# Gated delta rule block: projecting the four batches as two pairs, and storing each batch's decays with one transfer

## The chip, the cores and the metric

The kernel runs on one core of a Trainium2 chip, as one launch. The metric is the device time of that launch in microseconds (us). A core has five engines that each take their instructions in a fixed order: TensorE (PE, matmuls and transposes), VectorE (DVE), ScalarE (ACT), GpSimd (POOL) and SyncE (SP, which here only issues transfers). ACT and POOL issue transfers too; in the profile, the queue side of an engine carries a q (SPq, ACTq, POOLq). PE accumulates into PSUM, of which this kernel makes banks of 128 × 512 floats; everything else lives in SBUF, or is passed through tensors in device memory.

## The reference, cut to what matters

One transformer block over 4 batches of 512 tokens, 512 channels wide, all in float32: attention by a gated delta rule, then a gated feed-forward layer. Both are wrapped in a normalisation that is scaled and shifted by a modulation computed from a conditioning vector c.

```python
mod = (silu(c) @ wmod).reshape(4, 6, 1, 512)
sa, ca, ga, sb, cb, gb = (mod[:, i] for i in range(6))   # |ga|, |gb| at least 0.25
h = layernorm(x) * (1 + ca) + sa
x = x + ga * attention(h)
h = layernorm(x) * (1 + cb) + sb
x = x + gb * feed_forward(h)          # (silu(h Wg^T) * (h Wu^T)) Wd^T, 2048 hidden

def attention(h):
    q = short_conv(h @ Wq)            # causal, 4 taps, then silu: 6 heads x 64
    k = short_conv(h @ Wk)            # 6 heads x 64
    v = short_conv(h @ Wv)            # 6 heads x 128
    beta = sigmoid(h @ Wb)
    g = -exp(A_log) * softplus(h @ Wa + dt_bias)        # the decays
    q, k = l2norm(q) / 8, l2norm(k)
    # per head, token by token:
    #   S = S * exp(g);  S = S + k (beta * (v - k S));  o = q S
    o = rmsnorm(o) * norm_weight * silu(h @ Wg)
    return o @ Wo
```

## The kernel before, in words

The program is one function, `adaln_block`. It writes its work down stage by stage; a scheduler then fixes one order of instructions for each engine, and the engines keep to it, so a wait in front of one instruction holds up all that stand behind it on that engine. The order of the stages in the source is the main input to that order. The lists `steps` and `tails` hold small pieces of work that are put among larger ones: `between(h)` (called in the loops of `values` and `gates`) takes the next piece of the modulation, and `lagging` puts a block's last part one block later.

Four batches pass through these stages; the letters are the functions' own.

- `load_x` (L210–222) loads the four chunks of a batch's x, 128 tokens each. Batch 0 is loaded by SP, the others by ACT's queue. One of them has a tile of its own (`room`, a slot of the tag `hf`); the others take turns in four slots `xt`.
- `normed_t` (L275–296) normalises a batch on DVE (statistics at L272 and L273, scaling at L285), transposes it on PE (16 transposes `pxt`, L291), and applies the modulation on ACT (L292). The result is `ht`; three such tiles exist.
- `decays(bs, hts)` (L313–403) computes beta and g for several batches at once: a projection `pab` (L322 for one batch, L330 for several), transposes `pat` (L338), a chain of small ACT and DVE operations, a running sum `pd` (L383) by matmul, transposes `pgt` (L396) and a copy `gyt` (L398). ACT then stores g to `gd` and y to `yd`, in four transfers for each batch (L401 and L402).
- `keys` (L447–470), `queries` and `values` (L480–485) project by blocks of 128 output channels for each batch in the list they are given: four matmuls `pp_k`, `pp_q`, `pp_v` (L417), a scaled copy on ACT (L425), three convolution taps on DVE (L427), silu on ACT (L431). `squares` adds the norms: a square on ACT (L437) and small matmuls `pn` (L443). `values` also transposes v (`pvt`, L490) and scales it on DVE (L492). `gates` (L498–510) has matmuls `pp_g` and one activation on ACT (L504), no DVE. Every block's weights, 256 KB, are loaded once per call and block.
- The modulation (L163–203) is a matmul `pm` (L185), a copy `part` on DVE (L187), a fold `pmt` (L191) and rows `pmg` (L195).
- `triangles(b)` (L515–596) prepares the delta rule of a batch: it loads the decays back, spread over the partitions (`ec`, L521; `ex`, L545 and L549), multiplies keys with keys (L563), and inverts the triangular matrices by a chain of small DVE operations (`ti`, `tip`, L580–592), whose results are stored in `td` and `ttd` and loaded as `t` and `lm`.
- `delta_rule(b)` (L758 on) goes over the 4 chunks: `operands` (L600–670, matmuls L620, L648, L656, L663, products on DVE such as `yk` at L631), `scan` (L671–701: `pf`, `pm`, and `r` and `o` back and forth between PE, ACT and DVE), `finish` (squares and products on POOL at L715 and L721, sum on DVE at L717), `project` (`pwo` at L734, `xr` on POOL at L737).
- `weight_sums` (L785–798) loads feed-forward weights, adds them on POOL and stores the sums; `feed_forward` (L800–890) uses them.

PSUM is split into three banks `fill` for the projections, three banks `seq` for the steps of the delta rule, and a scratch of two halves.

The stages stand in the source in this order (`rest` is 1, 2, 3): batch 0 is normalised; keys and queries of 0; the loads of x1 and x2; values and triangles of 0; normalise 1 and 2; gates of 0; load and normalise 3; then

```python
    rest_betas = decays(rest, hts)
    delta_rule(0)
    weight_sums()
    keys(rest, hts)
    queries(rest, hts)
    complete()
    values([1], hts)
    gates([1], hts)
    triangles(1)
    values(rest[1:], hts)
    delta_rule(1)
    gates([2], hts)
```

and the gates of 3, followed by the feed-forward layers, with the triangles and delta rules of 2 and 3 among them. So batch 0 goes alone as far as its delta rule, and the keys and queries of the three others come together.

Of the kernel before, what the change touches and what calls it, by code (L numbers as in the profile page):

```python
# [19 lines left out]
NT = T // P  # L20
# [17 lines left out]
def adaln_block(  # L38
# [52 lines left out]
        return bank("seq", 3, name)  # L91


    kd, qd, vd, sd, gd, yd, xmid = ([] for _ in range(7))
    for b in range(B):
        kd.append(dr.tile([P, NP, T], F32, name=f"kd{b}"))
        qd.append(dr.tile([P, NP, T], F32, name=f"qd{b}"))
        vd.append(dr.tile([NT, P, H, DV], F32, name=f"vd{b}"))
        sd.append(dr.tile([NT, DV, H, P], F32, name=f"sd{b}"))
        gd.append(dr.tile([2, H, NT, C + 1], F32, name=f"gd{b}"))  # L100
        yd.append(dr.tile([2, H, NT, C], F32, name=f"yd{b}"))
        xmid.append(dr.tile([T, D], F32, name=f"xmid{b}"))
    wsum = [dr.tile([NF // 2, P, 7, 2, P], F32, name=f"wsum{i}") for i in range(2)]
    gate_d = dr.tile([2, B, D], F32, name="gate_d")
# [24 lines left out]
        out=upto, in_=upto, pattern=[[1, P]], compare_op=ALU.is_ge, fill=0.0, base=0,  # L129
        channel_multiplier=-1,  # L130
    )
    far = const.tile([2 * H, NT, 1], F32, name="far")
    pool.memset(far, FAR)

    start = const.tile([P, 2, NT, C + 1], F32, name="start")
# [73 lines left out]

    def load_x(b):  # L210
        ts = []
        if b == 2:

            room = w1.tile([P, NT, D], F32, tag="hf", bufs=2, name=f"xt{b}")
        for c in range(NT):
            if b == 2:
                t = room[:, c, :]
            else:
                t = pa_.tile([P, D], F32, tag="xt", bufs=4, name=f"xt{b}_{c}")
            (act if b else sp).dma_start(t, x[b, c * P : (c + 1) * P, :])  # L220
            ts.append(t)
        return ts
# [18 lines left out]
    nw = const.tile([P, 1], F32, name="nw")  # L241
    sp.dma_start(nw, norm_weight.rearrange("(p o) -> p o", o=1))
    for t in gd:
        sp.dma_start(t.rearrange("a h c i -> (a h) c i")[:, :, 0:1], far)


    kc, qc, lm1, t11, t22, xs = ([] for _ in range(6))
# [65 lines left out]
    def decays(bs, hts):  # L313

        m = len(bs)
        n = f"{bs[0]}"
        pab = (seq if bs == [0] else fill)(f"pab{n}")
        if m == 1:

            rows = P  # L320
            for k in range(KD):
                pe.matmul(  # L322
                    pab[k * S : (k + 1) * S, :], wab[:, k, :], hts[bs[0]][:, k, :],
                    start=True, stop=True,
                )
        else:
            rows = m * S
            for k in range(KD):
                for i, b in enumerate(bs):
                    pe.matmul(  # L330
                        pab[i * S : (i + 1) * S, :], wab[:, k, :], hts[b][:, k, :],
                        start=(k == 0), stop=(k == KD - 1),
                    )
        ab = pa_.tile([P, T], F32, tag="acc", bufs=4, name=f"ab{n}")[:rows]
        act.copy(ab, pab[:rows])
        pat = (seq if bs == [0] else fill)(f"pat{n}")
        for c in range(NT):
            pe.matmul(  # L338
                pat[:, c * P : c * P + m * S], ab[:, c * P : (c + 1) * P],
                fold if m == 1 else ident[:rows, :rows], start=True, stop=True,  # L340
            )
        pv = pat.rearrange("p (c b h) -> p b c h", b=P // S, h=S)[:, :m]

        def small(nm):
            return pa_.tile([P, 3, H, NT], F32, tag=nm, bufs=1, name=f"{nm}{n}")[:, :m]

        z, e, t, t2, beta = (small(i) for i in ("z", "e", "t", "t2", "beta"))
        s = e
        gy = pa_.tile([P, 3, 2, H, NT], F32, tag="gy", bufs=1, name=f"gy{n}")[:, :m]
        for i in range(m):  # L350
            vec.tensor_tensor(
                z[:, i], pv[:, i, :, 0:H].rearrange("p c h -> p h c"),
                dtb[:, :, None].broadcast_to([P, H, NT]), ALU.add,
            )
        act.activation(beta, pv[:, :, :, H : 2 * H].rearrange("p b c h -> p b h c"), AF.Exp, scale=-1.0)
        flat = [v.rearrange("p b h c -> p (b h c)") for v in (z, e, t, t2, s, beta)]
        fz, fe, ft, ft2, fs, fb = flat
        vec.tensor_scalar_add(fb, fb, 1.0)
        vec.reciprocal(fb, fb)


        vec.scalar_tensor_tensor(fe, fz, -1.0, fz, ALU.mult, ALU.max)
        act.activation(fe, fe, AF.Exp, scale=-1.0)
        vec.tensor_scalar_add(ft, fe, 2.0)
        vec.reciprocal(ft, ft)
        vec.tensor_mul(ft, ft, fe)
        vec.tensor_mul(ft2, ft, ft)
        vec.tensor_scalar_mul(fs, ft2, 1.0 / 17.0)
        for q in (15.0, 13.0, 11.0, 9.0, 7.0, 5.0, 3.0):
            vec.scalar_tensor_tensor(fs, fs, 1.0 / q, ft2, ALU.add, ALU.mult)  # L370
        vec.scalar_tensor_tensor(fs, fs, 1.0, ft, ALU.add, ALU.mult)
        vec.tensor_scalar_max(fz, fz, 0.0)
        vec.scalar_tensor_tensor(fs, fs, 2.0, fz, ALU.mult, ALU.add)
        g, y = gy[:, :, 0], gy[:, :, 1]
        for i in range(m):
            vec.tensor_tensor(
                g[:, i], s[:, i], neg_a[:, :, None].broadcast_to([P, H, NT]), ALU.mult
            )
            vec.tensor_scalar_max(g[:, i], g[:, i], G_FLOOR)
        pd = (seq if bs == [0] else fill)(f"pd{n}")  # L380
        hc = H * NT
        for i in range(m):
            pe.matmul(  # L383
                pd[:, i * hc : (i + 1) * hc], upto, g[:, i].rearrange("p h c -> p (h c)"),
                start=True, stop=True,
            )
        act.activation(
            y.rearrange("p b h c -> p b (h c)"), pd[:, : m * hc].rearrange("p (b c) -> p b c", b=m),
            AF.Exp,
        )  # L390
        for i, b in enumerate(bs):
            for par in range(2):
                r = slice(par * C, (par + 1) * C)
                pool.tensor_copy(y8[b][r, :, par::2], y[r, i])
            pgt = (seq if bs == [0] else fill)(f"pgt{b}")
            pe.transpose(pgt[: 2 * hc, :P], gy[:, i].rearrange("p a h c -> p (a h c)"), ident)  # L396
            gyt = pa_.tile([P, T], F32, tag="acc", bufs=4, name=f"gyt{b}")[: 2 * hc, :P]
            act.copy(gyt, pgt[: 2 * hc, :P])  # L398
            for a in range(2):
                own = slice(a * C, (a + 1) * C)  # L400
                act.dma_start(gd[b][a].rearrange("h c i -> (h c) i")[:, 1:], gyt[:hc, own])  # L401
                act.dma_start(yd[b][a].rearrange("h c i -> (h c) i"), gyt[hc:, own])  # L402
        return beta

    tails, pending = [], []
# [42 lines left out]
    def keys(bs, hts):  # L448
# [1 line left out]
        for i, b in enumerate(bs):  # L450
            sk[b] = pa_.tile([P, H, NT], F32, tag=f"sk{i}", bufs=1, name=f"sk{b}")
        for p in range(NP):
            w = first_w if bs == [0] and p == 0 else weight(w_k, p, f"k{bs[0]}_{p}")
            for b in bs:
                n = f"k{b}_{p}"
                kt = conv_silu(w, cw["k"], p, hts[b], n)
                act.dma_start(kd[b][:, p, :], kt)
                lagging(lambda a=(kt, sk[b], p, 1.0, n): squares(*a))
        betas = decays(bs, hts) if bs == [0] else rest_betas

        def scalars():
            for i, b in enumerate(bs):
# [16 lines left out]
    def values(bs, hts):  # L479
        for h in range(H):  # L480
            w = weight(w_v, h, f"v{bs[0]}_{h}")
            for b in bs:
                vt = conv_silu(w, cw["v"], h, hts[b], f"v{b}_{h}")
                lagging(lambda a=(b, h, vt): by_token(*a))
                between(h)

    def by_token(b, h, vt):
        pvt = fill(f"pvt{b}_{h}")
# [9 lines left out]
    def gates(bs, hts):  # L498
        for h in range(H):
            w = weight(w_g, h, f"g{bs[0]}_{h}")  # L500
            for b in bs:
# [5 lines left out]
                )  # L507
                if tails:
                    tails.pop(0)()
                between(h)  # L510


    ex, at, td, ttd, hf = {}, {}, {}, {}, {}
# [1 line left out]
    def triangles(b):  # L515
# [4 lines left out]
        for par in range(2):  # L520
            sp.dma_start(  # L521
                ec[par * C : (par + 1) * C].rearrange("p h c i -> p (h c i)"),
                gd[b][par].rearrange("h c i -> (h c i)").partition_broadcast(C),
            )
        kp = w1.tile([P, NP, T], F32, tag="kp", bufs=1, name=f"kp{b}")
        sp.dma_start(kp, kd[b])
# [16 lines left out]
        for par in range(2):  # L543
            tok = slice(par * C, (par + 1) * C)
            sp.dma_start(  # L545
                e[(1 - par) * C : (2 - par) * C, par].rearrange("p h c i -> p (h c i)"),
                yd[b][par].rearrange("h c i -> (h c i)").partition_broadcast(C),
            )
            sp.dma_start(  # L549
                e[tok, par].rearrange("p h c i -> p (h c) i"),  # L550
# [339 lines left out]
        down(NF // NQ - 1)  # L890


    hts = {0: normed_t(0, xts)}
    keys([0], hts)
    queries([0], hts)
    rest = list(range(1, B))
    xts = {b: load_x(b) for b in rest[:2]}
    loaded = []

    def step(j):  # L900
# [3 lines left out]
            loaded.append(modulation_load(j))  # L904

    steps.extend(lambda j=j: step(j) for j in range(2, 7))
    values([0], hts)
    triangles(0)
    for b in rest[:2]:
        hts[b] = normed_t(b, xts[b])  # L910
    gates([0], hts)
    for b in rest[2:]:
        hts[b] = normed_t(b, load_x(b))
    wo = const.tile([P, H, D], F32, name="wo")
    after(wo[:1, 0, :1])
    sp.dma_start(wo, w_o.rearrange("(h p) f -> p h f", p=P))
    rest_betas = decays(rest, hts)
    delta_rule(0)
    weight_sums()
    keys(rest, hts)  # L920
    queries(rest, hts)
    complete()
    values([1], hts)
    gates([1], hts)
    triangles(1)
    values(rest[1:], hts)
    delta_rule(1)
    gates([2], hts)
    complete()
    gates([3], hts)  # L930
# [60 lines left out]
```

## Time and profile before

| what | value |
|---|---|
| median of 3 runs | 1337.42 us (1333.15 to 1340.62) |
| profiled execution, its own time | 1337.62 us |
| its span, first to last instruction | 1335.4 us |
| mean granted clock of PE | 0.972 |
| busy: PE, DVE, ACT, POOL | 1249.2, 707.0, 390.8, 239.1 us |
| chain of work that ended last | PE 65%, DVE 13%, DMA 11%, POOL 4%, issue 4%, ACT 3% |
| DMA | 204.03 MB in 193,685 packets, 153 GB/s on average |

The profile is one execution. A group of its timeline gives start, length, engine, source line and operation; the bracket gives how long the engine had been idle before it, and what ended that. The granted clock is the share of full speed that PE was given; a digit 9 in the clock row means 90% or more.

### The profile page before, as it was taken

The page shows a single profiled execution, that of the slowest core. Times are in us where ns is not written, and L with a number is a line of the kernel's source. Part 1 is how long each engine was busy: PE and PEld are TensorE (multiplying, and loading weights), DVE is VectorE, ACT ScalarE, POOL GpSimd, SP SyncE. Part 2 cuts the span into 40 slices and gives each one's busy share as a digit, 9 for nine tenths or more (in the row PEclk, how much of TensorE's full clock was granted, in tenths as well). Part 3 has the DMA queues.
Part 4 walks back from the last instruction along what each step waited for, and adds up shares of the span by engine and source line. Part 5 has one row for each costly group of instructions (what it writes and reads, how often), then busy time and mean ns, then how long its engine had stood idle before and what let it go on. Part 6 is the DMA issues. An engine that isn't in the chain of part 4 may idle for free.

```text
span 1335.4 us, 17819 instructions
## 1 busy us (share of the span) xinstructions
PE 1249.2 (94%) x6608; PEld 783.4 (59%) x6608; DVE 707.0 (53%) x1549; ACT 390.8 (29%) x738; POOL 239.1 (18%) x274
## 2 busy tenths in 40 slices
PE   6798799899899999989999999999999999999998
PEld 3444455444444465657766666776666577576665
DVE  4665764355369444694435559543555444444443
ACT  3633266454224254222103332110244111011110
POOL 4010134443200011111112121011112110201102
PEclk9788799799999999999999999999999999999999
DMA  6569657576773536654325454533522333354331
GB/s 213 146 165 287 175 160 223 178 225 220 244 202 110 155 94 198 186 180 148 135 96 172 124 148 138 153 129 102 179 64 87 103 130 114 123 177 137 118 112 63
DMA packets 193685, 204.03 MB, mean 153 GB/s; under 512 B 81592, under 2 KB 150200, under 8 KB 193600
## 3 DMA queue, kind: packets, MB, share of 16 engines
q1 hardware_dynamic: 171744, 170.28, 42.6%
q10 hardware_dynamic: 19488, 17.93, 4.0%
q0 software_dynamic: 2368, 14.70, 2.8%
q8 instruction: 52, 0.85, 0.3%
q14 instruction: 33, 0.27, 0.1%
HBM read 152.94 MB, written 46.78 MB: 150 GB/s over the span
## 4 chain that ended last, share of the span: by engine, by line
PE 65%; DVE 13%; DMA 11%; POOL 4%; issue 4%; ACT 3%; SPq 0%; POOLq 0%; ACTq 0%; DVEq 0%
PE pd L827 15%; PE phg L854 12%; PE phu L854 10%; PE pwo L734 5%; PE pp_v L417 4%; PE pp_g L417 3%; PE pp_q L417 3%; PE pm L693 2%; DVE ti L591 2%; DVE tip L587 2%; DMA wu<-wsum 2%; DMA wsum<-wsg 2%; DMA wsum<-wsu 1%; PE scratch L620 1%; DMA xt<-in_x_dram 1%
## 5 line engine op out<-in xcount | busy, mean ns | idle before, releaser
L827 PE MATMUL pd<-wdn,hid 128*128 128x512 f32 x512 | 226.5, 595 | 3.6 <-DVE up L862 3.6
L833 POOL TENSOR_TENSOR xm<-xm,tmpf 128x512 f32<-128x512 f32 x64 | 81.1, 1267 | 478.5 <-DVE tmpf L832 478.5
L827 PEld LDWEIGHTS pd<-wdn,hid 128*128 128x128 f32 x512 | 97.7, 191 | 113.8 <-issue 103.4
L854 PE MATMUL phg<-hf,wg 128*128 128x256 f32 x512 | 136.4, 384 | 3.5 <-DMA wg<-wsum 2.0
L854 PEld LDWEIGHTS phg<-hf,wg 128*128 128x128 f32 x512 | 95.6, 191 | 25.1 <-issue 7.7
L854 PE MATMUL phg<-hs,wg 128*128 128x256 f32 x384 | 101.2, 385 | 3.2 <-DVE hid L861 3.1
L832 DVE TENSOR_TENSOR tmpf<-pd,gb 128x512 f32<-128x512 f32 x64 | 44.1, 690 | 104.1 <-PE pd L827 93.0
L854 PE MATMUL phu<-hf,wu 128*128 128x256 f32 x384 | 97.2, 381 | 1.3 <-ACT up L859 0.9
L734 PE MATMUL pwo<-wo,ot 128*128 128x512 f32 x192 | 94.9, 624 | 0.6 <-DVE ot L731 0.6
L854 PE MATMUL phu<-hs,wu 128*128 128x256 f32 x384 | 94.4, 381 | 0.5 <-DVE up L867 0.5
L417 PE MATMUL pp_v<-ht,wv 128*128 128x512 f32 x192 | 91.6, 621 | 2.7 <-DVE v L492 2.3
L417 PE MATMUL pp_g<-ht,wg 128*128 128x512 f32 x192 | 91.0, 614 | 1.6 <-issue 1.5
L859 ACT COPY hid<-phg 128x256 f32<-128x256 f32 x32 | 11.9, 372 | 257.8 <-PE phg L854 257.7
L854 PEld LDWEIGHTS phu<-hs,wu 128*128 128x128 f32 x384 | 72.0, 190 | 19.0 <-DVE up L867 6.0
L854 PEld LDWEIGHTS phg<-hs,wg 128*128 128x128 f32 x384 | 70.8, 191 | 17.2 <-DVE hid L861 4.2
L854 PEld LDWEIGHTS phu<-hf,wu 128*128 128x128 f32 x384 | 72.1, 190 | 12.4 <-ACT up L859 1.7
L417 PEld LDWEIGHTS pp_v<-ht,wv 128*128 128x128 f32 x192 | 36.1, 198 | 42.7 <-issue 39.7
L427 DVE SCALAR_TENSOR_TENSOR acc_v<-pp_v,conv_v,acc_v 128x511 f32<-128x511 f32 (+2 forms) x72 | 53.4, 744 | 9.6 <-ACT acc_v L425 8.7
L417 PEld LDWEIGHTS pp_g<-ht,wg 128*128 128x128 f32 x192 | 35.1, 194 | 38.4 <-issue 37.2
L417 PE MATMUL pp_k<-ht,wk 128*128 128x512 f32 x96 | 51.4, 662 | 4.2 <-DVE acc_k L427 4.2
L883 ACT ACTIVATE hid<-hid 128x1024 f32<-128x1024 f32 x32 | 33.8, 1057 | 72.0 <-DVE hid L867 64.6
L693 PE MATMUL pm<-r,l 128*128 128x128 f32 x384 | 53.4, 287 | 1.2 <-ACT r L689 1.2
(215 smaller groups left out, 1797.6 us busy)
## 6 DMA issues: line engine op xcount, KB each, us to landing
wg<-wsum SPq DMA_DIRECT2D x32, 896.0 KB
wu<-wsum SPq DMA_DIRECT2D x32, 896.0 KB
wdn<-in_w_down_t_dram SPq DMA_DIRECT2D x32, 512.0 KB
wsum<-wsg POOLq DMA_DIRECT2D x8, 896.0 KB, 4.1
wsum<-wsu POOLq DMA_DIRECT2D x8, 896.0 KB, 5.1
vd<-v SPq DMA_DIRECT2D x24, 256.0 KB
wg<-in_w_g_dram SPq DMA_DIRECT2D x24, 256.0 KB
sd<-sg ACTq DMA_DIRECT2D x24, 256.0 KB
```

The source lines that it names most:

```text
L417: pe.matmul(pp, w[:, k, :], ht[:, k, :], start=(k == 0), stop=(k == KD - 1))
L427: vec.scalar_tensor_tensor(acc[:, i:], pp[:, : T - i], taps[:, col, TAPS - 1 - i : TAPS - i], acc[:, i:], ALU.mult, ALU.add,)
L587: vec.tensor_tensor(v, pm[:, j, j + 1 :, None].broadcast_to([n, m, j]), t[:, j : j + 1, :j].broadcast_to([n, m, j]), ALU.mult,)
L591: vec.tensor_add(t[:, j + 1 :, :j], t[:, j + 1 :, :j], v)
L620: pe.matmul(pv[:, u, 2 * par : 2 * par + 2, :], kc[i][us, p, par : par + 2, :], qc[i][us, p, par : par + 2, :], start=True, stop=True,)
L693: pe.matmul(pm[:, h], l[:, hs.start + h, 2 * par : 2 * par + 2, :], r[:, par, hs.start + h], start=True, stop=True,)
L734: pe.matmul(pw, ot[:, h, :], wo[:, h, :], start=(h == 0), stop=(h == H - 1))
L827: pe.matmul(pd, hids[q, i // 2][:, i % 2, c * P : (c + 1) * P], wdn[q, i // 2][:, i % 2, :], start=(i == 0), stop=(i == NQ - 1),)
L832: vec.tensor_mul(tmp, pd, gb)
L833: pool.tensor_add(xm[c], xm[c], tmp)
L854: pe.matmul(o, l[:, k], r[:, k], start=k == 0, stop=k == 1)
L883: act.activation(hid, hid, AF.Silu)
```

## The change

Batches 0 and 1 are now normalised first, and their keys, queries and values are computed together, block by block; batch 1's x is loaded at the start into the tile `room`. The keys and queries of batches 2 and 3 come together between the first and the second delta rule, and their values behind the second. The gates of batch 1 and its triangles come straight behind the first delta rule in the source. The decays are computed for batches 0 and 1 together, and for 2 and 3 together. g and y of a batch are one tensor `gd` in device memory, written with one transfer; `yd` is gone. Each head's row in it begins with a constant, set at the start from `far` in two transfers for each batch, and `ex` is loaded around that constant, 64 values at a time. `between(h)` is called once for a block, not once for a block and batch. What is computed stays the same.

```diff
-        gd.append(dr.tile([2, H, NT, C + 1], F32, name=f"gd{b}"))
-        yd.append(dr.tile([2, H, NT, C], F32, name=f"yd{b}"))
+        gd.append(dr.tile([2, 2, H, NT, C + 1], F32, name=f"gd{b}"))
...
-    far = const.tile([2 * H, NT, 1], F32, name="far")
+    far = const.tile([H, NT, 1], F32, name="far")
...
-        if b == 2:
+        if b == 1:
 
             room = w1.tile([P, NT, D], F32, tag="hf", bufs=2, name=f"xt{b}")
         for c in range(NT):
-            if b == 2:
+            if b == 1:
                 t = room[:, c, :]
             else:
                 t = pa_.tile([P, D], F32, tag="xt", bufs=4, name=f"xt{b}_{c}")
...
     for t in gd:
-        sp.dma_start(t.rearrange("a h c i -> (a h) c i")[:, :, 0:1], far)
+        for a in range(2):
+            sp.dma_start(t[a, 0, :, :, 0:1], far)
...
-        pab = (seq if bs == [0] else fill)(f"pab{n}")
+        pab = (seq if 0 in bs else fill)(f"pab{n}")
...
             act.copy(gyt, pgt[: 2 * hc, :P])
-            for a in range(2):
-                own = slice(a * C, (a + 1) * C)
-                act.dma_start(gd[b][a].rearrange("h c i -> (h c) i")[:, 1:], gyt[:hc, own])
-                act.dma_start(yd[b][a].rearrange("h c i -> (h c) i"), gyt[hc:, own])
+            act.dma_start(
+                gd[b].rearrange("a g h c i -> (g h c) a i")[:, :, 1:],
+                gyt.rearrange("p (a i) -> p a i", a=2),
+            )
...
-        betas = decays(bs, hts) if bs == [0] else rest_betas
+        betas = decays(bs, hts) if 0 in bs else rest_betas
...
                 lagging(lambda a=(b, h, vt): by_token(*a))
-                between(h)
+            between(h)
...
                     tails.pop(0)()
-                between(h)
+            between(h)
...
-                gd[b][par].rearrange("h c i -> (h c i)").partition_broadcast(C),
+                gd[b][par, 0].rearrange("h c i -> (h c i)").partition_broadcast(C),
...
-                e[(1 - par) * C : (2 - par) * C, par].rearrange("p h c i -> p (h c i)"),
-                yd[b][par].rearrange("h c i -> (h c i)").partition_broadcast(C),
+                e[(1 - par) * C : (2 - par) * C, par].rearrange("p h c i -> p (h c) i"),
+                gd[b][par, 1].rearrange("h c i -> (h c) i")[:, 1:].partition_broadcast(C),
...
-    hts = {0: normed_t(0, xts)}
-    keys([0], hts)
-    queries([0], hts)
-    rest = list(range(1, B))
-    xts = {b: load_x(b) for b in rest[:2]}
+    xts = {0: xts, 1: load_x(1)}
+    hts = {b: normed_t(b, xts[b]) for b in (0, 1)}
+    keys([0, 1], hts)
+    xts[2] = load_x(2)
+    queries([0, 1], hts)
...
-    values([0], hts)
     triangles(0)
-    for b in rest[:2]:
-        hts[b] = normed_t(b, xts[b])
+    values([0, 1], hts)
     gates([0], hts)
-    for b in rest[2:]:
-        hts[b] = normed_t(b, load_x(b))
+    for b in (2, 3):
+        hts[b] = normed_t(b, xts[b] if b in xts else load_x(b))
...
-    rest_betas = decays(rest, hts)
+    rest_betas = decays([2, 3], hts)
     delta_rule(0)
     weight_sums()
-    keys(rest, hts)
-    queries(rest, hts)
-    complete()
-    values([1], hts)
     gates([1], hts)
     triangles(1)
-    values(rest[1:], hts)
+    keys([2, 3], hts)
+    complete()
+    queries([2, 3], hts)
     delta_rule(1)
+    values([2, 3], hts)
     gates([2], hts)
     complete()
     gates([3], hts)
```

More of the change, by code (lines that the diff above doesn't have):

```diff
@@ L91, in seq @@
         return bank("seq", 3, name)
-    kd, qd, vd, sd, gd, yd, xmid = ([] for _ in range(7))
+    kd, qd, vd, sd, gd, xmid = ([] for _ in range(6))
     for b in range(B):
@@ L335, in decays @@
         act.copy(ab, pab[:rows])
-        pat = (seq if bs == [0] else fill)(f"pat{n}")
+        pat = (seq if 0 in bs else fill)(f"pat{n}")
         for c in range(NT):
@@ L379, in decays @@
             vec.tensor_scalar_max(g[:, i], g[:, i], G_FLOOR)
-        pd = (seq if bs == [0] else fill)(f"pd{n}")
+        pd = (seq if 0 in bs else fill)(f"pd{n}")
         hc = H * NT
@@ L394, in decays @@
                 pool.tensor_copy(y8[b][r, :, par::2], y[r, i])
-            pgt = (seq if bs == [0] else fill)(f"pgt{b}")
+            pgt = (seq if 0 in bs else fill)(f"pgt{b}")
             pe.transpose(pgt[: 2 * hc, :P], gy[:, i].rearrange("p a h c -> p (a h c)"), ident)
@@ L452, in keys @@
         for p in range(NP):
-            w = first_w if bs == [0] and p == 0 else weight(w_k, p, f"k{bs[0]}_{p}")
+            w = first_w if 0 in bs and p == 0 else weight(w_k, p, f"k{bs[0]}_{p}")
             for b in bs:
```

## The prediction

> **What bounds the kernel now.** I read the page first. TensorE (PE) is busy 94% of the span, VectorE (DVE) 53%: what the change can win or lose is PE's idle time, 86 us in all, and time in which PE is busy but slow.
>
> ```profile
> PE 1249.2 (94%) x6608; PEld 783.4 (59%) x6608; DVE 707.0 (53%) x1549; ACT 390.8 (29%) x738; POOL 239.1 (18%) x274
> ...
> PEclk9788799799999999999999999999999999999999
> ...
> q1 hardware_dynamic: 171744, 170.28, 42.6%
> ```
>
> The clock row is low in the first third only, where the change is made. So I cut the span at the stage borders and took busy times by engine. The columns are: stretch, its length, then PE, PE's weight loads, DVE, ScalarE (ACT), GpSimd (POOL), granted clock, DMA share, GB/s.
>
> ```profile
> 0.00:24.00 24.00, 12.97 (x51) 7.24 (x51) 7.38 (x18) 7.56 (x11) 13.61 (x48) 1.00 0.73 225
> 24.00:62.30 38.30, 31.45 (x162) 15.85 (x161) 26.22 (x70) 22.62 (x32) 0.69 (x3) 0.85 0.48 146
> 62.30:143.00 80.70, 73.19 (x323) 35.68 (x322) 51.62 (x107) 26.89 (x39) 9.85 (x15) 0.86 0.77 222
> 143.00:168.00 25.00, 18.04 (x132) 10.75 (x130) 14.79 (x57) 6.19 (x16) 1.38 (x7) 0.73 0.57 163
> 168.00:280.00 112.00, 101.77 (x790) 58.80 (x789) 59.31 (x123) 66.12 (x118) 49.44 (x60) 0.92 0.61 195
> 280.00:450.00 170.00, 162.54 (x655) 77.02 (x653) 104.21 (x196) 58.95 (x92) 27.07 (x38) 1.00 0.66 198
> 450.00:600.00 150.00, 138.45 (x986) 90.45 (x987) 89.53 (x215) 54.20 (x113) 22.32 (x17) 0.98 0.55 159
> ```
>
> They are: first loads and batch 0's normalise; its keys and queries; its values, the modulation, gates of batch 0; start of delta rule 0; its body, with the other batches' keys; their queries and values; delta rule 1. From 600 us on (PE 711 of 735) the change touches nothing.
>
> Then PE's timeline, for what ended the idle time before a group (in brackets).
>
> ```profile
> 38.53 1.02 PE L443 MATMUL pn_k<-sel,sq_k 128*64 128x2 f32 x16 [2.98 <-ACT sq_k L437]
> ...
> 42.29 6.38 PE L417 MATMUL pp_q<-ht,wq 128*128 128x512 f32 x8
> ...
> 61.39 1.02 PE L443 MATMUL pn_q<-sel,sq_q 128*64 128x2 f32 x16 [3.70 <-ACT sq_q L437]
> 62.34 6.59 PE L417 MATMUL pp_v<-ht,wv 128*128 128x512 f32 x8
> ...
> 78.54 3.70 PE L417 MATMUL pp_v<-ht,wv 128*128 128x512 f32 x8 [0.18 <-DVE v L492]
> ...
> 120.34 1.84 PE L191 MATMUL pmt<-fold,part 128*128 128x4 f32 x8 [2.95 <-DVE part L187]
> ...
> 155.61 1.62 PE L648 MATMUL scratch<-t,at 64*64 64x32 f32 x24 [2.84 <-DMA t<-td]
> ...
> 246.77 6.53 PE L417 MATMUL pp_k<-ht,wk 128*128 128x512 f32 x8 [4.16 <-DVE acc_k L427]
> ```
>
> The same eight matmuls take 3.70 us in a steady stretch and 6.4 to 6.6 us after a pause: a wait costs itself and about 2.8 us more on the next block, often some on the one behind. Adding idle and excess per stretch, I get these losses before: 11 us to 24; 15 in 24–62; 16 in 62–143; 10 in 143–168; 18 in 168–280; 7.5 in 280–450; 15.6 in 450–600.
>
> Last, DVE's and ACT's timelines for who stands in front:
>
> ```profile
> 113.96 0.70 DVE L272 BATCH_NORM_STATS2 st<-xt 128x6 f32<-128x512 f32 x1 [10.90 <-DMA xt<-in_x_dram]
> ...
> 245.11 0.95 DVE L717 TENSOR_REDUCE ms<-osq 128x6 f32<-128x768 f32 x1 [7.21 <-POOL osq L715]
> ```
>
> ```profile
> 13.05 0.21 ACT L237 ACTIVATE neg_a<-neg_a 128x6 f32<-128x6 f32 x1 [0.62 <-DMA neg_a<-in_a_log_dram]
> 13.49 3.21 ACTq L220 DMA_DIRECT2D xt<-in_x_dram  x3
> ```
>
> At 113.96 DVE waits for x, at 245.11 for POOL, and acc_k and PE stand behind the second one.
>
> **The change part by part.** Arithmetic is the same but for decays, so each part is a change of loss. Plus is slower. I read where each instruction stands on its in-order engine from the new order of instructions.
>
> *Start, +4.5.* x1 is loaded first and DVE does its BatchNorm statistics ahead of batch 0's normalise. Its last chunk is issued after neg_a on ACT, at 16.4 us (three issues end at 16.7); with some 4 us of landing and 4×0.7 us of DVE, x0 is normalised near 22.5 instead of 18.8. Batch 1's 16 transposes (2.4 us of PE) come in before the keys. pp_k starts near 29.6 instead of 24.0; less those 2.4 us, 3.2, and some 1.5 of slow matmuls.
>
> *Keys and queries by pairs, −0.5 (−3 to +3).* Two batches' blocks in turn hide the 2.98 us wait for sq_k and the decay chain (pd waits some 0.4). But ACT runs the squares of q behind the next block's silu: pn_q waits about 6.7 us, with 3 to 5 after it at half speed. Loss 14.5 against 15.
>
> *Values [0,1] and gates 0, +7 (0 to +15).* batch 0's triangle chain (60 DVE operations of 0.35 us, 21 us) now stands among the value convolutions. Seven blocks cost DVE 3×0.75 + 0.69 us each and the chain beside it, 38 us, against 33 us of PE (3.63 + pvt and modulation): 5 us. pmt and pmg wait behind that DVE work for 3.5+3.6+3+1 = 11 us instead of 6. Loss 23 against 16.
>
> *Start of delta rule 0, +6.7 (−4 to +12).* The triangles are long done, so the 2.84 and 3.00 us waits for t and yk go. But x3 finds its slots only when batch 2's transposes are done and ACT has copied them out. Before, the chain of waits shows x's DMA for 6.20 us from 108.37 to the first chunk, about 19 us pass from issue to a normalised batch, and some 30 us were there until its transposes at 141; now its 16 transposes stand between the first matmuls of pf. I put 6 to 7 us of wait there, 2 to 3 for the decays' pd and pgt behind it (no projection lies between), 5 of slow clock. Loss 17 against 10.
>
> *Body of delta rule 0, −8 (−14 to +2).* Its filler was the keys of three batches (nine blocks of four pp_k, each with a convolution on DVE); now it is the gates of batch 1 (six blocks of four pp_g, 6×3.6 = 21 us, with ACT alone). The row at 245.11 no longer stops PE through acc_k: 4.16 us of wait and 7.6 of slow blocks go. Against it, less filler: 21 us for scan steps that wait on DVE and POOL. Loss 10 against 18.
>
> *Keys and queries [2,3] with triangles 1, +1 (0 to +5):* DVE 61 us, PE 58; before, the values of [2,3] held such a chain and lost 7.5.
>
> *Delta rule 1 to the feed-forward, −1 (−3 to +3).* Values [2,3] and gates 2 and 3 cover it; its tail loses part of that cover. 14.5 against 15.6.
>
> *Decays, +2.7.* pab is now paired for batches 0 and 1 (8 matmuls of 512 columns each: near 4.5 us against 1.79 + 1.06 less what is shared); the other pair costs 3.63 like the three before.
>
> *Transfers, 0 (−2 to +5).* One store instead of four takes some 1.5 us off ACT's queue per batch (issues of 0.3 to 0.55 us). Six weight loads of 256 KB go. `far` costs SP four more issues of about 0.5 us. ex is loaded in runs of 256 bytes instead of one long run per partition: 1,536 packets in each of 8 loads. A packet of q1 takes 0.426×1335.4/171,744 = 3.3 ns of all 16 engines on average, 5 us a load. It is wanted tens of us later, under the value blocks; without that cover, +5 once.
>
> Sum 4.5−0.5+7+6.7−8+1−1+2.7 = +12.4 on the profiled execution's 1337.6 us (span 1335.4 and 2.2 around it; the median of the runs is 1337.4): **1350 us**.
>
> **Two rules against rows.** *Clock.* PE has 2.98 us idle at 38.53, then small matmuls, then a block at 6.38 instead of 3.70; after other pauses, such as the 4.16 us, the slowdown lasts 7 to 14 us. The Trainium skill (TensorE: Matmul & The Clock Gate, "HAM oscillation") has only gaps over about 3.4 us count, and Part 1 has 3.4 us of work bring the clock back. By that, delta rule 0 would gain back 1.7 us of slow matmuls and not 7.6, and the sum be near +18. I take the trace's price. *Runs.* The row of q1 gives 5 us a load; DMA: Bandwidth & Descriptors ("Specifications") says that below 512 bytes the engine reads, modifies and writes, so the rate falls. At its 435 GB/s halved, 384 KB would take 1.8 us, an estimate from that page. It speaks against the 256-byte loads, but under either the transfer is hidden: the sum stays. No row of before shows this pattern, so I keep 0.
>
> **The rivals.**
> *Faster, 1323 us.* x3 lands in time and DVE keeps up among the values: start +3, keys −0.5, values 0, start of delta rule −4 (its two waits gone, nothing for them), body −13, end −3, decays +2.7: −14.8. For it: 18 us of loss in the body really stem from work that leaves it. Against: x's slow loads (10.90 at 113.96). It decides at the transposes of batch 3: chunks there within 5.5 us of the end of batch 2's, or not.
> *No change, about 1337.* Body −13, values +3, start of the delta rule +3, the rest as above: −0.3.
> *Much slower, 1372.* DVE is the bound of values (+15), the decays' chain follows x3's delay (+12), and delta rule 0, with 21 us of filler, pauses in each scan step and never regains its clock (+2): +35. For it: clock 0.73 and 0.92 there before. Against: gates need no DVE.
> *The change doesn't do what it says:* the schedule could pull work back over the stages. In the order, the triangles stand among values and gates 1 in delta rule 0, so hardly.
>
> **How the numbers follow.** This kernel's measurement can tell about 0.5%, 6.7 us, from no change. Forecast 0.44 (1344 to 1360, slower), much slower 0.18, no change 0.17 with the case that it does nothing, faster 0.21. So slower 0.62, same 0.17, faster 0.21. The range, 1321 to 1377, leaves out half of the fastest case and a third of the slowest.
>
> **What would show it.** Start: pp_k near 29.6. Pairs: no wait on sq_k, one near 6.7 on sq_q. Values: pmt and pmg waiting on DVE's part, with ti among the rows. Delta rule 0: a wait of pxt for xt's DMA or DVE ahead of pf, none for t; later no pp block of 6.5 us and no wait on acc_k. A wait on ex would make the transfers wrong; pxt without a wait and a body of 100 us or less, the forecast.

## The result, and the profile after

The changed kernel takes 1350.88 us (median of 4 runs, 1350.01 to 1352.93). The kernel before, run beside it, takes 1335.29 us. The ratio of the two is 1.0112, with a 95% interval of 1.0075 to 1.0148. The profiled execution of after has a span of 1348.2 us, against 1335.4.

Page of the changed kernel, the same rows as before (busy time and share by engine; granted clock in 40 slices; the main queue with packets, MB and its share of the 16 engines):

```profile
PE 1246.4 (92%) x6608; PEld 783.3 (58%) x6608; DVE 708.8 (53%) x1549; ACT 389.2 (29%) x736; POOL 242.8 (18%) x274
...
PEclk9989898999898999799999999999999999999999
...
q1 hardware_dynamic: 180352, 168.71, 42.1%
```

PE's busy time is 2.8 us less and its idle time 15.6 us more; that is the 12.8 us of span. The question is where the idle time lies. The first border is the same point of delta rule 0 in both programs (all 96 of its `pm` and 36 of its 48 `pwo` matmuls lie ahead of it), though different other work is done by then, and the first feed-forward is under way at 600 or 620 us. First before, then after (stretch, length, busy time of PE, its loads, DVE, ACT, POOL, granted clock, DMA share, GB/s):

```profile
0.00:280.00 280.00, 237.41 (x1448) 128.32 (x1449) 159.32 (x373) 129.38 (x215) 74.97 (x132) 0.88 0.64 196
280.00:600.00 320.00, 300.99 (x1641) 167.47 (x1640) 193.74 (x411) 113.15 (x205) 49.39 (x55) 0.99 0.61 179
```

```profile
0.00:297.20 297.20, 254.94 (x1472) 135.20 (x1472) 167.86 (x379) 120.56 (x207) 63.82 (x116) 0.93 0.63 184
297.20:620.00 322.80, 286.07 (x1631) 162.33 (x1631) 189.48 (x409) 121.88 (x213) 66.13 (x72) 0.93 0.59 176
```

Length less PE's busy time gives 42.6 us idle before and 42.3 after in the first part, at a better clock after (0.93 against 0.88). In the second part it is 19.0 us before and 36.7 after, at a worse clock (0.93 against 0.99). **The whole loss lies behind delta rule 0.** The forecast had put it ahead of that.

Idle time alone does not say how much work was done. Here is the first stretch again, with the matmuls of the projections (L417) alone: their busy time on PE and their count, then the clock and the transfers of the stretch. First before, then after, with one steady run of such matmuls from after:

```profile
0.00:280.00 280.00, 119.09 (x222) 0.88 0.64 196
```

```profile
0.00:297.20 297.20, 141.63 (x288) 0.93 0.63 184
...
505.43 13.90 PE L417 MATMUL pp_g<-ht,wg 128*128 128x512 f32 x32
```

At the same point of delta rule 0, the changed kernel has done 66 more of these matmuls. At 13.90 / 32 = 0.43 us each they are worth some 29 us (an estimate), and it took 17 us more: it stands some 11 us ahead. At 607.0 us before and 621.7 after, the same 3,505 matmuls are left in both. (The other matmuls that differ in number, such as 24 pvt more and 32 pn fewer, are small and come out about even.) From border to border, then, the changed kernel had 29 us less of work and took 2.5 us less time: some 26 us are lost behind delta rule 0, more than the whole slowdown.

The waits of PE that matter, from its timeline in the changed kernel:

```profile
77.36 1.02 PE L443 MATMUL pn_q<-sel,sq_q 128*64 128x2 f32 x16 [6.97 <-ACT sq_q L437]
78.31 6.11 PE L417 MATMUL pp_q<-ht,wq 128*128 128x512 f32 x8
...
131.82 1.87 PE L194 MATMUL pmg<-part,fold 128*4 128x512 f32 x2 [2.81 <-DVE part L186]
133.62 5.77 PE L417 MATMUL pp_v<-ht,wv 128*128 128x512 f32 x8
...
156.30 1.87 PE L190 MATMUL pmt<-fold,part 128*128 128x4 f32 x8 [3.50 <-DVE part L186]
...
197.01 1.49 PE L656 MATMUL scratch<-t,xs 64*64 64x32 f32 x24 [5.03 <-ACT xs L652]
...
333.59 1.02 PE L443 MATMUL pn_k<-sel,sq_k 128*64 128x2 f32 x16 [5.16 <-ACT sq_k L437]
...
405.36 0.42 PE L648 MATMUL scratch<-t,at 64*64 64x32 f32 x2 [5.76 <-DMA t<-td]
...
563.46 2.05 PE L854 MATMUL phg<-hf,wg 128*128 128x256 f32 x4 [5.78 <-DMA wg<-wsum]
```

The rows up to 197.01 lie ahead of delta rule 0's body; the windows above show them made up for by its end. The last three have nothing like them in the kernel before. The row at 333.59 goes back to DVE, which stands at the head of batch 1's triangles until a transfer lands, with the convolution of k behind it:

```profile
329.10 1.28 DVE L580 COPY ti<-pm 96x1024 f32<-96x1024 f32 x1 [6.75 <-DMA pm<-ad]
330.31 0.73 DVE L427 SCALAR_TENSOR_TENSOR acc_k<-pp_k,conv_k,acc_k 128x510 f32<-128x510 f32 x1
```

At 405.36 delta rule 1 wants the inverse of the same triangles, which has not been stored and loaded back yet. At 563.46 the first feed-forward starts with nothing beside it. In the source, the projections' buffers are given up behind the last gates, and the loads of the feed-forward come after that. In after, SP's queue waited 12.4 us for the last pp_g, until 546.2, and issued wg at 556.17, behind four stores for batch 2's triangles. In the kernel before, the last pp_g came earlier, wg was issued at 524.62, and the last chunks of delta rule 1 lay in that hole:

```profile
450.60 0.30 PE L648 MATMUL scratch<-t,at 64*64 64x32 f32 x2 [1.57 <-DMA t<-td]
...
515.53 1.88 PE L417 MATMUL pp_g<-ht,wg 128*128 128x512 f32 x4
...
537.16 1.03 PE L854 MATMUL phg<-hf,wg 128*128 128x256 f32 x4
```

The row at 450.60 is delta rule 1's first use of t. Of the 96 gate matmuls that the profile counts for batches 2 and 3, 54 ran ahead of it in the kernel before and 42 beside the delta rule or behind; in after, all 96 come behind it. This is the scheduler's order: in the source of before, too, both gate calls stand behind `delta_rule(1)`.

### The profile page after: what moved, and what is told of

Its sections match the earlier page's. It is cut to its first block, busy times and chain, and to the rows that moved or that the text cites. A ratio compares the mean times of both kernels' runs of the same rounds, so it can differ in the third digit from the quotient of the medians.

```text
span 1348.2 us, 17784 instructions
## 1 busy us (share of the span) xinstructions
PE 1246.4 (92%) x6608; PEld 783.3 (58%) x6608; DVE 708.8 (53%) x1549; ACT 389.2 (29%) x736; POOL 242.8 (18%) x274
## 4 chain that ended last, share of the span: by engine, by line
PE 67%; DVE 12%; DMA 9%; POOL 4%; issue 4%; ACT 2%; SPq 1%; POOLq 0%; ACTq 0%; DVEq 0%
PE pd L827 14%; PE phg L854 12%; PE phu L854 10%; PE pp_v L417 6%; PE pwo L734 5%; PE pp_g L417 4%; PE pp_q L417 2%; PE pm L693 2%; PE pp_k L417 2%; DVE ti L591 2%; DMA wsum<-wsu 1%; PE pf L684 1%; DVE tip L587 1%; DMA wu<-wsum 1%; PE scratch L620 1%
## 5 line engine op out<-in xcount | busy, mean ns | idle before, releaser
L417 PE MATMUL pp_v<-ht,wv 128*128 128x512 f32 x192 | 96.8, 636 | 0.4 <-DVE acc_v L427 0.3
L417 PE MATMUL pp_g<-ht,wg 128*128 128x512 f32 x192 | 91.7, 619 | 0.2 <-ACT sg L504 0.2
L417 PEld LDWEIGHTS pp_g<-ht,wg 128*128 128x128 f32 x192 | 35.6, 197 | 37.6 <-issue 36.8
L417 PEld LDWEIGHTS pp_v<-ht,wv 128*128 128x128 f32 x192 | 35.0, 199 | 33.2 <-issue 32.0
L734 PEld LDWEIGHTS pwo<-wo,ot 128*128 128x128 f32 x192 | 34.6, 194 | 32.8 <-issue 30.1
```

The lines of the kernel that those rows point to most:

```text
L417: pe.matmul(pp, w[:, k, :], ht[:, k, :], start=(k == 0), stop=(k == KD - 1))
L734: pe.matmul(pw, ot[:, h, :], wo[:, h, :], start=(h == 0), stop=(h == H - 1))
```

## The experiments

**The order around delta rule 1.** The first run undoes one pair of calls:

```diff
-    delta_rule(1)
     values([2, 3], hts)
+    delta_rule(1)
     gates([2], hts)
```

> Only the order of two calls is undone: values([2,3]) before delta_rule(1), as before, instead of behind it. After stands at 1350.9. Theory A (read from the trace of after: the loss sits behind 297 us, in a delta rule 1 that starts before its triangles are ready, t<-td 5.76 us, and in a feed-forward that starts at 563 us with nothing beside it, 16 us idle from 545 to 620): the values cover the triangles, delta rule 1 with the gates covers the change to the feed-forward; the t wait is under 2 us, the idle time from the last gates to the first pd under 10 us; 1337 to 1342. Rival B (the forecast's account: the loss is in the start, the values of 0 and 1 and the start of delta rule 0, all ahead of 226 us): within 2 us of after, 1349 to 1353.

1345.51 us, ratio to before 1.0079 (1.0056 to 1.0102): less than after by 5 us of median, with intervals that overlap. The wait for t is gone, but the hole at the feed-forward is not: the gates still outlast delta rule 1.

```profile
555.72 2.05 PE L854 MATMUL phg<-hf,wg 128*128 128x256 f32 x4 [6.06 <-DMA wg<-wsum]
```

So theory A was half right, and its own number was missed. Only 8 of the 96 gate matmuls ran ahead of delta rule 1's first use of t in this run, so one call put back in the source did not bring back the order of instructions. The next run moves one of the two gate calls ahead as well, which makes 52 of 96:

```diff
-    delta_rule(1)
     values([2, 3], hts)
     gates([2], hts)
+    delta_rule(1)
     complete()
     gates([3], hts)
```

> As e1_values_first, with gates([2]) moved ahead of delta_rule(1) too, so that less of the gates is left when delta rule 1 ends and its last chunks can lie beside the first feed-forward, as before. Theory A (the feed-forward starts with nothing beside it: 6.06 us on wg and some 7 us on the triangles' at and yk in e1, at 543 to 556 us): these waits fall under 5 us together, 6 to 10 us less than e1, 1336 to 1340. Rival: delta rule 1 only loses filler, what is won at the feed-forward is lost in its scan, 1343 to 1348.

1336.51 us, ratio 1.0013 (0.9991 to 1.0034): level with before, and clear of after's interval. Nothing else of the change was taken back. Windows of this run, at the borders of delta rule 1 and the feed-forward:

```profile
299.80:452.00 152.20, 137.60 (x632) 66.18 (x630) 96.66 (x190) 58.07 (x93) 40.41 (x53) 0.96 0.67 210
452.00:560.00 108.00, 101.70 (x841) 62.83 (x840) 49.03 (x112) 45.71 (x98) 17.61 (x13) 0.98 0.50 140
560.00:620.00 60.00, 55.39 (x224) 40.43 (x224) 47.62 (x120) 12.82 (x23) 10.42 (x7) 1.00 0.65 196
```

```profile
537.85 1.03 PE L854 MATMUL phg<-hf,wg 128*128 128x256 f32 x4
```

phg starts at 537.85 without a wait, as it did before, and the idle time from 299.8 to 620 is 25.5 us instead of 36.7. So the place of delta rule 1 among the values and gates, in the order of instructions, is the cause of the slowdown. The level total is still a sum: counted as above, this run is some 9 us ahead of before at 299.8 us, the same point of delta rule 0, and loses some 9 from there to the same border in the feed-forward (607.2 us).

**Triangles of batch 1 earlier.** In after, they stand behind the gates of batch 1:

```diff
-    gates([1], hts)
     triangles(1)
+    gates([1], hts)
```

> triangles(1) stands before gates([1]) behind the first delta rule, so its work gets in earlier by some blocks; nothing else moves in the source. Theory A: the 6.75 us that DVE waits at 329 us for pm<-ad (behind which acc_k, sq_k and PE's 5.16 us stand) and the 5.76 us t<-td wait shrink, 5 to 9 us less, 1342 to 1346; the idle time at the start of the feed-forward stays. Rival B: nothing behind 226 us costs, within 2 us of after.

1360.86 us, ratio 1.018 (1.0138 to 1.0223): 10 us of median over after, though the two intervals just overlap, and against both theories. The wait for t shrank only to 4.50 us, though it came 10 us sooner. PE instead waits for DVE elsewhere (7.87 us for ot at 343), and the feed-forward's first part came out in another order of instructions and took 51.3 us from phg to pd instead of 43.7. Earlier triangles do not help while the values stand behind delta rule 1.

**x3 earlier.** Batch 3's x gets the second slot of `hf`:

```diff
-        if b == 1:
+        if b in (1, 3):
...
-            if b == 1:
+            if b in (1, 3):
                 t = room[:, c, :]
...
     xts[2] = load_x(2)
+    xts[3] = load_x(3)
     queries([0, 1], hts)
```

> x3 gets the second slot of the tag hf as its own tile and is loaded right behind x2, so that it no longer waits for batch 2's slots. Rival B (forecast: 6.7 us at the start of delta rule 0 for x3): the 5.03 us wait on xs and the slow clock behind it go, 5 to 8 us less, 1343 to 1346. Theory A (PE idles there only 3.6 us longer than before, and ACT, not pxt, was what waited): 3 to 5 us less, 1346 to 1348; the time behind 297 us stays as it is.

1349.08 us, ratio 1.0098 (1.0063 to 1.0132): not to be told from after. The stall itself went. In after it came from ACT's queue, where two issues of x3 waited for slots, ahead of xs:

```profile
192.09 4.13 ACTq L219 DMA_DIRECT2D xt<-in_x_dram  x2
196.32 0.64 ACT L652 COPY xs<-scratch 64x192 f32<-64x192 f32 x2 [3.86 <-DMA xt<-in_x_dram]
```

This is the stretch of the start in after, then the same stretch with x3 early:

```profile
188.90:226.00 37.10, 26.46 (x267) 19.41 (x265) 19.80 (x53) 17.20 (x36) 9.53 (x15) 0.82 0.64 201
```

```profile
188.90:226.00 37.10, 34.31 (x281) 22.76 (x280) 11.57 (x40) 15.88 (x35) 8.31 (x16) 0.82 0.63 182
```

Idle time falls by 7.9 us (10.6 to 2.8), but delta rule 1 meets its wait for t at 402.89 instead of 405.36. More than half was given back on the way; within delta rule 0, PE now waits 3.33 us for yk at 254 (1.16 in after).

**What stands in delta rule 0's body.** In after, the gates of 1 and the triangles behind them go back behind the queries:

```diff
-    gates([1], hts)
-    triangles(1)
     keys([2, 3], hts)
     complete()
     queries([2, 3], hts)
+    gates([1], hts)
+    triangles(1)
     delta_rule(1)
```

> After with gates([1]) and triangles(1) moved back behind the queries of 2 and 3, so that the keys are delta rule 0's filler again. The forecast's step (body of delta rule 0: 8 us won by having gates there): 8 to 12 us more than after, 1359 to 1363, with DVE's wait for POOL's osq and PE's for acc_k back between 226 and 300 us. Rival (the triangles of batch 1 come no later than before and no longer hold up the keys' convolutions, so the waits at 329 and 405 us go in exchange): within 4 us of after, 1347 to 1355.

1355.42 us, ratio 1.0167 (1.0116 to 1.0218): 4.5 us of median over after, with overlapping intervals. It lies just outside both ranges and does not tell the theories apart. The waits of 7.21 and 4.16 us from the kernel before do not come back, though the keys do. The same question in the kernel before:

```diff
     weight_sums()
+    gates([1], hts)
     keys(rest, hts)
     queries(rest, hts)
     complete()
     values([1], hts)
-    gates([1], hts)
```

> The kernel before, with nothing changed but that gates([1]) stands ahead of keys(rest), so that delta rule 0 has gates beside it. Before stands at 1334 to 1335. The forecast's step says 8 us less, the trace of after (idle time 10.2 us before, 2.3 after in this stretch) up to 10: 1324 to 1328. Rival: the key blocks, which come in any case, now meet POOL's late finish or the triangles further on, and nothing is won: 1333 to 1337.

1338.75 us, ratio 1.0013 (0.998 to 1.0046): nothing won. The waiting only changed its place, and again it is for POOL:

```profile
252.73 0.90 PE L730 MATMUL pot<-ident,o 128*128 128x128 f32 x3 [8.79 <-POOL o L721]
```

So, in the order of before, gates beside the delta rule are no better than keys, and the suspect is POOL. In `weight_sums` it waits at the head of its order for loads (5 to 7 us each in the kernel before), and osq and o of the delta rule stand behind. The next run takes the sums out of delta rule 0 and leaves the keys in:

```diff
     delta_rule(0)
-    weight_sums()
     keys(rest, hts)
     queries(rest, hts)
     complete()
+    weight_sums()
...
                 w = pa_.tile([P, 7, 2, P], F32, tag="wm", bufs=1, name=f"ws{nm}{i}")
+                if i == 0 and nm == "g":
+                    after(w[:1, 0, 0, :1])
```

> The kernel before with weight_sums() behind the queries of the others, its first load held back until the last query is through, so that POOL has nothing but its own work in delta rule 0; the keys stay there as filler. Before stands at 1336. If the loss in that stretch came from POOL waiting for the sums' weights (6 to 7 us each, osq then 7.21 us late on DVE, acc_k 4.16 us on PE): 8 to 12 us less, 1324 to 1328. If it came from the keys' convolutions, as the forecast had it: within 3 us, 1333 to 1339. The sums could be late for the feed-forward, which would show as a wait on wsum.

1346.9 us, ratio 1.0084 (1.0056 to 1.0112): slower in the end, but its delta rule 0 clears the keys.

```profile
163.00:260.00 97.00, 96.63 (x800) 56.69 (x799) 59.56 (x124) 62.43 (x114) 19.94 (x17) 1.00 0.33 97
260.00:340.00 80.00, 80.00 (x351) 38.20 (x352) 41.08 (x71) 31.60 (x54) 11.27 (x19) 1.00 0.57 178
340.00:450.00 110.00, 82.78 (x290) 38.56 (x288) 66.33 (x125) 26.55 (x39) 36.02 (x48) 0.86 0.77 244
```

```profile
375.88 0.69 DVE L492 TENSOR_TENSOR v<-pvt,nk 128x512 f32<-128x512 f32 x1 [13.49 <-DMA vd<-v]
```

From 163 to 340 us PE is idle for 0.4 us, with key convolutions beside the delta rule, at full clock; the last pp_q starts at 293.12 instead of 313.24. The sums' transfers left this stretch together with POOL's additions (DMA share 0.33 in the first row, 0.61 in the kernel before), and no run tells the two apart. In after, the sums stand in delta rule 0 as they did before, and POOL waits up to 10.12 us for their loads, yet osq holds DVE for 3.67 us at most:

```profile
281.94 0.95 DVE L717 TENSOR_REDUCE ms<-osq 128x6 f32<-128x768 f32 x1 [3.67 <-POOL osq L715]
```

Why the sums fall better there is not shown. In b3_sums_later, all of the 20 us, and more, are then lost among the values, where DVE waits for v's buffer to be stored. Is that SP's queue, in which the sums' loads wait for their slot ahead of v's stores? The last run loads them through POOL's queue:

```diff
                 for a in range(2):
-                    sp.dma_start(
+                    pool.dma_start(
                         w[:, 2 * a : 2 * a + 2].rearrange("p h k f -> p (h k) f"),
```

> b3_sums_later with the sums' weights loaded through POOL's own queue instead of SP's. In b3 PE is busy 176.6 of 177 us from 163 to 340 us, and the last pp_q starts at 293.1 us instead of 313.2 as before; then v waits 13.5 us on the store vd<-v, 11 us over the kernel before at the end. If that is because the sums' loads stand in SP's queue waiting for their slot, ahead of v's stores: the waits on vd go, and most of the 20 us stays, 1316 to 1324 (before 1335). If it is the DMA engines' own load (0.77 busy there), or POOL late for the triangles of batch 1: no better than b3, 1340 to 1347.

1365.24 us, ratio 1.0259 (1.0222 to 1.0295): the number was missed by far. The waits on vd did go, and delta rule 1 asked for t at 433.16 instead of 453.99, so SP's queue was what held v up. But the sums were not through by then, and POOL's place in delta rule 1 was behind them:

```profile
501.87 1.23 PE L620 MATMUL scratch<-qc,kc 64*128 64x128 f32 x8 [38.99 <-ACT lm L668]
```

```profile
500.13 0.95 DVE L717 TENSOR_REDUCE ms<-osq 128x6 f32<-128x768 f32 x1 [40.60 <-POOL osq L715]
```

It is the same wait as in delta rule 0 of the kernel before, 40.60 instead of 7.21 us. A place for the sums that is free of it was not found.

**Triangles of batch 0 late.** On top of e5_gates2_before_dr1, they stand behind the values again:

```diff
-    triangles(0)
     values([0, 1], hts)
+    triangles(0)
     gates([0], hts)
```

> e5_gates2_before_dr1 (1336.5) with triangles(0) behind values([0,1]) again, as the triangles stood behind the values before; nothing else. The forecast's step for values (7 us, from the triangles' chain among the convolutions and pmt, pmg waiting behind it): 4 to 8 us less, 1329 to 1333, with PE's 6.97 us wait for sq_q also shorter, since the scans of the triangles leave the queries. Rival: the triangles are then late for delta rule 0, which waits for t (2.84 us before, and 22 us of gates as the only cover): within 3 us of e5 or slower, 1334 to 1342.

1346.11 us, ratio 1.0083 (1.0052 to 1.0114): 10 us slower than e5, intervals apart. The values run freely, and batch 3's normalise, behind the triangles on DVE, is late instead:

```profile
195.47 2.93 PE L291 MATMUL pxt<-ident,xt 128*128 128x128 f32 x12 [15.39 <-DVE xt L285]
...
209.01 1.27 PE L648 MATMUL scratch<-t,at 64*64 64x32 f32 x18 [3.13 <-DMA t<-td]
```

The wait for sq_q did not move (6.98 us); the scheduler left one scan of the triangles among the queries in this order too, so this part stays untested.

**The store of the decays.** Three runs: after with the four stores of before, the kernel before with the one store of after, and e5 with four stores. The edit, here in the direction of the first and third (the tensors, `far` and the loads of ex change with it and are left out here):

```diff
-            act.dma_start(
-                gd[b].rearrange("a g h c i -> (g h c) a i")[:, :, 1:],
-                gyt.rearrange("p (a i) -> p a i", a=2),
-            )
+            for a in range(2):
+                own = slice(a * C, (a + 1) * C)
+                act.dma_start(gd[b][a].rearrange("h c i -> (h c) i")[:, 1:], gyt[:hc, own])
+                act.dma_start(yd[b][a].rearrange("h c i -> (h c) i"), gyt[hc:, own])
```

> The decays are stored as before: gd and yd apart, four transfers a batch, ex loaded in long runs. The rest is as in after. Both theories (the forecast put 0 on this part, -2 to +5): within 2 us of after, 1349 to 1353. If the 256-byte runs were on the path: 3 to 5 us less.

> The kernel before, with nothing changed but the decays' storage: one transfer a batch into the joint gd, ex loaded in 256-byte runs, far in eight transfers. The forecast put 0 on it (-2 to +5): 1332 to 1339. Rival, from e4_two_stores (18 us slower than after with four stores): the four stores hold up ACT's queue wherever they stand, and one store wins 5 us or more, below 1330.

> e5_gates2_before_dr1 (1336.5) with the decays stored as before, in four transfers a batch. e4_two_stores was 18 us slower than after; of that its trace shows some 4 to 8 us ahead of 200 us and 8 in the first feed-forward, whose instructions stand in another order there. If the stores themselves cost (eight of them together on ACT's queue, ahead of sq_q and the convolutions): 4 to 8 us more, 1340 to 1345. If the order was all: within 2 us, 1334 to 1339. If 18 us come again: 1352 to 1357.

1369.32 us, ratio 1.025 (1.0212 to 1.0288), far over after. 1338.49 us, ratio 1.003 (1.0005 to 1.0056), hardly over before. 1350.29 us, ratio 1.0107 (1.0066 to 1.0148), clear of e5. In the paired order the one store is worth some 14 to 18 us, in the order of before nothing. What is direct of it can be seen in ACT's timeline, first e5, then e5 with four stores:

```profile
69.88 0.81 ACTq L399 DMA_DIRECT2D gd<-gyt  x2
70.74 1.84 ACT L425 ACTIVATE acc_q<-pp_q,conv_q 128x512 f32<-128x512 f32 x3 [0.73 <-ACT gyt L398]
```

```profile
72.39 1.84 ACT L425 ACTIVATE acc_q<-pp_q,conv_q 128x512 f32<-128x512 f32 x3 [3.41 <-DMA gd<-gyt]
```

Eight stores in a row keep ACT for 3.4 us, two for 0.7, and PE's wait for sq_q goes from 6.97 to 9.14 us. The rest comes later: with four stores the scheduler also wrote delta rule 0 in another order, in which PE waits 2.80, 1.47 and 3.21 us for DVE and POOL at 269, 297 and 323 us. That this reordering is the rest is argued; no run isolates it. Two other things change with the stores, the loads of ex in long runs and four issues fewer of `far`, and no run separates them either.

## Why the prediction was right or wrong

The total was right (1350 forecast, 1350.9 measured), the account of it was not: two errors of some 25 us cancelled, which is luck. The terms up to the end of delta rule 0 summed to +12.4, and the changed kernel is some 11 us ahead there. The terms behind it summed to 0, and some 26 us were lost there.

- *Start, +4.5:* the mechanism held. pp_k started at 28.94 (29.6 forecast), PE waited 3.06 us for x0's normalise, idle time rose by 2.7 us. No slow matmuls followed, so the term was 2 us too large.
- *Keys and queries by pairs:* held. The wait on sq_k is gone, the one on sq_q is 6.97 us (6.7 forecast), with a block at 6.11 behind it.
- *Values of 0 and 1, +7:* **failed.** Between 98.9 and 147 us DVE was busy 39 of 48 us, and the convolutions with the triangles between them kept up; pmt and pmg waited 7.1 us in sum (2.81, 3.50, 0.57, 0.25) and not 11. Idle time from 78.3 to 188.9 us was 8.0 us, with far more work in it than the 7.5 before and at a better clock (0.92 against 0.86). Where it was tried, on top of e5_gates2_before_dr1, taking the early triangles back cost 10 us. The estimate took one run of seven blocks for the whole stretch; by its own figures DVE's part is 7 × 2.94 + 21 = 42 us, not 38, further still from what was measured.
- *Start of delta rule 0, +6.7:* the place and x3 were right, the waiting instruction was not. The transposes of x3 never waited; ACT spent 4.13 us on two issues of x3 that waited for slots, and xs stood behind them (5.03 us on PE). Idle time rose by 3.7 us, not 6.7 (10.6 in 37 us against 7.0 in 25), and without the stall the program ended hardly sooner.
- *Body of delta rule 0, −8:* the direction was right and the gain larger: idle time alone fell by 7.9 us (2.3 against 10.2), and the clock rose (0.97 against 0.92). The cause was wrong. It named the keys' convolutions. In the kernel before, gates in place of keys won nothing, and keys without the sums left PE idle for 0.4 us, so the loss there came with the weight sums. What spared after, which keeps the sums, stays open.
- *Keys and queries [2,3], +1, and delta rule 1 to the feed-forward, −1:* **failed, and this is the slowdown.** Idle time from 297 to 620 us is 17.7 us over that of before (36.7 against 19.0), and the clock is lower (0.93 against 0.99). The step reasoned that values and gates cover delta rule 1. It did not ask what covers the start of the first feed-forward when delta rule 1 ends before the gates, nor what is left for batch 1's triangles when the values no longer stand ahead of delta rule 1.
- *Decays, +2.7:* near. pab of the pair took 1.04 + 1.05 + 1.91 + 1.04 = 5.0 us against 2.85, which is +2.2, and the second pair 3.63 as forecast. The step's own figures, 4.5 against 2.85, give +1.7 and not +2.7.
- *Transfers, 0:* right for the 256-byte loads of ex, on which PE never waited. For the store, 0 holds in the order of before only.

Of the two rules, the clock's (the Trainium skill, TensorE: Matmul & The Clock Gate, "HAM oscillation") can be read again: 2.81 us idle at 131.82, below the rule's 3.4, and the block behind it takes 5.77 us instead of 3.60. The trace's price was the better one. The rule on short runs decided nothing. Of the rivals, the fast one was right that delta rule 0's body would run almost without waits, and that the values would cost nothing more. No case had the loss behind it; with the order of instructions around delta rule 1 brought back, the kernel is level with before, where the no-change case had it.

## What to carry to other kernels

A sum over stages can be right by accident: check each term against idle time by stage, with the borders put where the work of both kernels is alike, and count the work done up to each border. The order of calls in the source is not the order of instructions: read where a stage stands on its engine. When a stage is moved ahead, ask what it used to cover at its old place, above all at a change of buffers, where the next stage's loads can't start before the last user is through. An in-order engine that waits at its head for a transfer (here POOL for weights, DVE for triangles, ACT and SP for slots) held up whatever stood behind it, for 4.13 us in one place and for 40.60 in another; moving that work moved the wait.

## What was not expected

Four stores instead of one, small by their own length (2.7 us more of ACT), cost 14 to 18 us in one order of the stages and none in the other. And the body of a delta rule, with its chains of small matmuls, kept PE busy for 96.6 of 97 us at full clock (163 to 260 us in b3_sums_later), where the weight sums had been moved out of it.
